# Two heads of scores ahead of each group's products, and four smaller moves, in a cross-attention kernel

## The chip, the cores and the metric

The kernel runs on one NeuronCore of one Trainium2 chip. The metric is the device time of one execution, in microseconds (us). Before the change it is 429.61 us, the median of three runs (429.59 to 430.12).

The engines are named as in the profile: PE is TensorE's matrix multiply and PEld its loading of weights, DVE is VectorE, ACT is ScalarE, POOL is GpSimd and SP is SyncE, which here only issues DMA transfers.

## The reference

Eight batches of 112 query rows with 320 channels attend to 375 context rows of 512 features, with 20 heads of 16 channels. The last four context rows are prompt tokens, with keys and values of their own. Cut to what matters:

```
q        = heads(x @ W_q)
probs_t  = softmax(q @ heads(text @ W_k)^T * scale)           # 371 text rows
text_out = probs_t @ heads(text @ W_v)
qsem     = l2norm(probs_t @ text)                             # 512 wide, per head
sem      = qsem @ l2norm(ip)^T                                # 4 prompt rows
fused    = q @ heads(ip @ W_k_ip)^T * scale + 0.5 * sem
probs_ip = softmax(fused) * spatial_mask
ip_out   = probs_ip @ heads(ip @ W_v_ip)
out      = (text_out + ip_out) @ W_out + b_out + x
```

## The kernel before, in words

All arithmetic is float32. A head is never expanded to 512 features: the norm of `qsem` comes from the Gram matrix of the context. For one head the kernel multiplies the unnormalised probabilities by a matrix `u` whose columns are a triangle of the Gram matrix, the four prompt columns, a column of ones and the head's 16 values. One product of up to 392 columns so gives, in one PSUM bank `ps_qd`, everything that the head needs.

The 40 steps are pairs (b, g) of a batch and a group of four heads. The four heads of a group use the four strips of 32 rows of TensorE's array, head `a` on strip `a`. A step consists of:

- `scores` (line 676): one product of 32 rows by 375 columns for a head, on the strip of that head, into a PSUM bank `ps_s`. In float32 each product appears as two instructions.
- `probabilities` (line 705): VectorE takes the negative maximum `nmx` (L709), ScalarE the exponential `p` (L712) and copies the prompt logits `ipl` (L714), and `sent` (line 718) has SyncE put `p` into another layout `xg`.
- `transposed` (line 725): VectorE transposes `xg` to `xgT` (L729).
- `multiplied` (line 735): twelve blocks (the index `j`) of four products (L748). After each block the generator yields, and other work is written in between.
- `value_sums` (L761, ScalarE) and `reduced` (L794, VectorE) read the four banks `ps_qd`, after which the next group may use them.

The loop over the steps (line 1207) works two steps ahead. During step n it writes the scores of heads 2 and 3 of step n + 2 (`now`) after block 0, and those of heads 0 and 1 (`then`) after block 6. Their probabilities follow at once for `now` and after the products for `then`. In two steps of the second to last batch other heads are also written after block 0 (`more`).

After the products of a step, `between(b, g)` (line 1079) writes pieces of the next batch's work: its Gram matrix, its values (`ps_v`, L578, copied by L585), its keys (`ps_k`, L544, copied by L551; the third chunk is transposed by L535 and copied by L540), the projected queries (`project_queries`: transposes L333, copies L336, projections L344, masked copies `qm` on VectorE, L353), and `finish` of the batch before (the transposes `ps_a`, L950, copied by L954, and the projection `ps_o`, L962). For the first batch `prompt_logits` (L665, copied by L672) belongs to these too.

PSUM has eight banks, dealt out in three pools: four for `ps_qd`, two for scores (`ps_sc`) and two common ones (`ps_mm`). `bank(name)` takes a common one and `bank(name, spare=True)` one of the two for scores. Each pool hands its banks out in turn, so a tile waits until the last reader of the tile two before it (in these pools of two) has finished.

The instructions of TensorE, SyncE, VectorE and (in the loop) ScalarE run in the order in which they are written; a wait in front of one holds back those that are written after it on its engine. GpSimd's are ordered by the planner. GpSimd's copy L655 (`placed`) puts a group's values `vr` into `u`; these come from DRAM (L603, `values_to_groups`, after step (b, 3)), where SyncE stored them (L594).

Of the kernel before, what the change touches and what calls it, by code (L numbers as in the profile page):

```python
# [20 lines left out]
def kernel(  # L21
# [16 lines left out]
    B, S, C = x.shape  # L38
# [10 lines left out]
    FULL = C // P  # L49
# [11 lines left out]
    NG = H // GROUP  # L61
# [23 lines left out]
    def bank(name, spare=False):  # L85

        if spare:
            return ps_sc.tile([P, 512], F32, tag="sc", name=name)
        return ps_mm.tile([P, 512], F32, tag="mm", name=name)
# [223 lines left out]
    pairs = [[0]] + [list(range(b, min(b + 2, B))) for b in range(1, B, 2)]  # L313
# [211 lines left out]
    def keys(b):  # L525
        s = st[b]
        if b > 0:
            nc.gpsimd.tensor_copy(s["kT"][:, :, TT:], kip[:, :, b * NIP : (b + 1) * NIP])
        for i in range(NC):
            ps = bank(f"ps_k_{b}_{i}", spare=0 < b < B - 1 and i == FULL)  # L530
            if 0 < b < B - 1 and i == FULL:

                for c in range(NT):
                    rows = min(P, TT - c * P)
                    nc.tensor.transpose(  # L535
                        ps[:, c * P : c * P + rows],
                        s["k3"][:rows, c].rearrange("p a r d -> p (a r d)"),
                        ident[:rows, :rows],
                    )
                nc.scalar.copy(s["kT"][:, i, :TT], ps[:, :TT])  # L540
                yield
                return
            for e in range(NE):
                nc.tensor.matmul(  # L544
                    ps[:, :TT],
                    wk_sb[:, e, i * P : (i + 1) * P],
                    s["ctxT"][:, e, :TT],
                    start=(e == 0),
                    stop=(e == NE - 1),
                )  # L550
            nc.scalar.copy(s["kT"][:, i, :TT], ps[:, :TT])  # L551
            yield
# [382 lines left out]
    def prompt_sums_and_projection(b, s, eng, part, n, h0, i0, i1, w, attn, ah):  # L935
        wv = work.tile([S, NIP, H, D], F32, tag="wv", name=f"wv_{b}_{h0}", bufs=1)[:, :, :n]
        eng.tensor_tensor(  # L937
            wv,
            s["vip"][:, :, part],
            w.rearrange("p h n -> p n h").unsqueeze(3).to_broadcast([S, NIP, n, D]),  # L940
            ALU.mult,
        )
        eng.tensor_tensor(wv[:, :2], wv[:, :2], wv[:, 2:], ALU.add)
        eng.tensor_tensor(ah, ah, wv[:, 0], ALU.add)
        eng.tensor_tensor(ah, ah, wv[:, 1], ALU.add)
        yield

        ps = bank(f"ps_a_{b}_{h0}", spare=True)
        for i in range(i0, i1):
            nc.tensor.transpose(  # L950
                ps[:, i * S : (i + 1) * S], attn[:, i * P : (i + 1) * P], ident[:S, :S]
            )
        aT = work.tile([P, NC, S], F32, tag="aT", name=f"aT_{b}_{h0}")
        nc.scalar.copy(  # L954
            aT[:, i0:i1], ps[:, i0 * S : i1 * S].rearrange("p (i s) -> p i s", s=S)
        )
        yield

        s["o"] = bank(f"ps_o_{b}")
        ps = s["o"]  # L960
        for i in range(i0, i1):
            nc.tensor.matmul(  # L962
                ps[:S, :C], aT[:, i, :], wo_sb[:, i, :], start=(i == 0), stop=(i == NC - 1)
            )
        yield
# [106 lines left out]
    def run(key, make, pieces=1):  # L1072

        if key not in gens:
            gens[key] = make()
        for _ in range(pieces):
            next(gens[key], None)

    def between(b, g):

        nb = b + 1
        new = nb < B


        first = [bs for bs in pairs if bs[0] == (nb if b == 0 else nb + 1)]
        rest = [bs for bs in pairs if bs[0] == nb]
        if g == 0:
            if new:
                run(("g", nb), lambda: gram(nb), 2)
            if new:  # L1090
                run(("g", nb), None)
            if b == 0:
                run(("v", nb), None)
            if b > 0 and new:
                run(("f", b - 1), lambda: finish(b - 1))
        if g == 1:
            if new:
                run(("v", nb), lambda: values(nb), 1 if b == 0 else 2)
            if b == 0:
                run(("pp",), prompt_projections)  # L1100
            for bs in first if b == 0 else ():
                run(("q", bs[0]), lambda: project_queries(bs), 3)
        if g == 2 and new:
            run(("v", nb), None)
            run(("k", nb), lambda: keys(nb))
            for bs in first if b == 0 else ():
                run(("q", bs[0]), None)
        if g == 2 and b > 0 and new:
            run(("f", b - 1), None, 2)
        if g == 3:  # L1110
            if new:
                run(("k", nb), None, 1)
            if b > 0 and new:
                run(("f", b - 1), None)
            for bs in first if b > 0 else ():
                run(("q", bs[0]), lambda: project_queries(bs), 3)
            if b == 0:
                run(("t", b), lambda: prompt_logits(b))
            for bs in rest:
                run(("q", bs[0]), None)  # L1120
        if g < NT and nb + 1 < B:
            run(("c", nb + 1), lambda: transposed_context(nb + 1))
        if g == 4:
            if b > 0 and new:
                run(("f", b - 1), None, 2)
            if nb < B - 1:
                run(("k", nb), None, 1)
            for bs in (first if b > 0 else []) + (rest if b < B - 2 else []):
                run(("q", bs[0]), None)

    prompts = normalised_prompts()
    context = transposed_context(0)
# [62 lines left out]
    def ahead(n):  # L1195

        c, d = steps[n + LEAD : n + LEAD + 2]
        if steps[n] == (B - 2, NG - 2):
            todo = ((c, 2, 3), (c, 0, 1), (d, 2, 3))
        elif steps[n] == (B - 2, NG - 1):  # L1200
            todo = ((c, 0, 1), (d, 2, 3), (d, 0, 1))
        else:
            todo = ((c, 2, 3), (c,), (c, 0, 1))
        return [[(t[0], a) for a in t[1:]] for t in todo]

    ctx.enter_context(tc.manual_schedule(engines=engines | {mybir.EngineType.Activation}))
    for n, (b, g) in enumerate(steps[:-NG]):
        now, more, then = ahead(n)
        for j, _ in enumerate(multiplied(b, g)):
            if j == 0:  # L1210
                for c, a in now:
                    scores(*c, a)
                    probabilities(*c, a)
                for c, a in more:
                    scores(*c, a, ps=bank(f"ps_s_{c[0]}_{c[1]}_{a}"))
                    probabilities(*c, a, hold=True)
            if j == 6:
                for c, a in then:
                    scores(*c, a)
            if j == 2:  # L1220
                if g == 0:
                    gram_banks(b + 1)
                transposed(*steps[n + 1])
                for c, a in more:
                    sent(*c, a)
                if 1 <= g <= 3:
                    gram_to_groups(b + 1, {1: (0,), 2: (2,), 3: (3,)}[g])

                if g in (1, 2) and b > 0:
                    run(("f", b - 1), None)  # L1230
        value_sums(b, g)
        if g == 2 and b > 0:
            run(("f", b - 1), None)
        for c, a in then:
            probabilities(*c, a)
        if n == len(steps) - NG - 1:
            sums = shared(b, g, GROUP // 2)
            next(sums)
            reduced(b, g, 2)
        else:  # L1240
            reduced(b, g)
        placed(*steps[n + 1])
        if g == 0 and b > 1:
            run(("f", b - 2), None)
        load_rest(n)
        if g == NG - 1:
            load_next(b + 3)
        if g == 1:
            gram_to_groups(b + 1, (1,))
        elif g == 3:  # L1250
            values_to_groups(b + 1)
        if g in (2, 3) and b == 0:
            run(("pp",), None)
        if (b, g) == (B - 3, 1):
            prompt_values_by_head()
        if (b, g) == (B - 2, 1):
            bd = load_prompt_values_by_head()
        if g == NG - 1 and b < B - 2:
            prompt_values(b)
        between(b, g)  # L1260
        if g == 1:
            values_to_dram(b + 1, nc.sync, 0, 2)
        if g == 2:
            values_to_dram(b + 1, nc.sync, 2)
# [10 lines left out]
    b = B - 1  # L1275
# [126 lines left out]
```

## Time and profile before

| | us |
|---|---|
| median of three runs | 429.61 |
| profiled execution | 429.75 |
| its span, first to last instruction | 428.0 |
| TensorE busy (share of the span) | 419.5 (98%) |
| VectorE busy | 327.8 (77%) |
| ScalarE busy | 189.7 (44%) |
| GpSimd busy | 111.1 (26%) |
| products `ps_qd`, busy time of TensorE | 221.7 |
| scores `ps_s` | 65.5 |
| values `ps_v` | 63.6 |
| keys `ps_k` (L544) | 46.3 |

A line of a timeline gives the start and the busy time in us, the engine, the line of the code, the operation, what it writes and reads, the size of the first of the instructions that the line merges and their count; in brackets stands the idle time of the engine before it and what ended it. A matmul is pipelined and its end is modelled, so a busy TensorE is not one at its peak. The view of the waits gives for a pair "who waits <- for whom" the sum in us, how many times, and the longest. The granted clock of TensorE was 0.999 of full speed.

### The profile page before, as it was taken

How to read it: one execution, taken by the hardware profiler on the slowest of the kernel's cores; microseconds unless marked ns; L12 is line 12 of the kernel's file. 1: busy time of each engine (PE TensorE's matmuls, PEld its weight loads, DVE VectorE, ACT ScalarE, POOL GpSimd, SP SyncE). 2: the span in 40 equal slices, each digit the busy share in tenths (PEclk: the TensorE clock that was granted, in tenths of full speed). 3: DMA queues.
4: the chain of work that ended last, by engine and by line, in shares of the span. 5: the costliest groups of instructions: out<-in, count | busy, mean ns of one | idle time of the engine just before them, and what ended most of it. 6: DMA issues, size and time to landing. Idle time of an engine off the chain costs nothing.

```text
span 428.0 us, 13975 instructions
## 1 busy us (share of the span) xinstructions
PE 419.5 (98%) x5521; PEld 330.3 (77%) x5521; DVE 327.8 (77%) x672; ACT 189.7 (44%) x659; POOL 111.1 (26%) x275
## 2 busy tenths in 40 slices
PE   8999999989999999999999999999999999999995
PEld 8867768878777877789777977788777887687993
DVE  5038569787887879788797878887788977889873
ACT  2344342346334353345435363334634363446773
POOL 5310101112060212411152121511133120515550
PEclk9999999999999999999999999999999999999999
DMA  8776665687645956476646956468556536564200
GB/s 239 199 192 211 140 169 157 160 200 149 166 123 138 207 152 179 123 162 150 168 121 160 189 124 170 127 153 175 141 166 153 145 96 173 156 159 121 65 2 27
DMA packets 57630, 64.26 MB, mean 150 GB/s; under 512 B 18448, under 2 KB 51592, under 8 KB 57566
## 3 DMA queue, kind: packets, MB, share of 16 engines
q1 hardware_dynamic: 56934, 62.42, 58.2%
q8 instruction: 43, 0.70, 0.8%
q10 hardware_dynamic: 632, 0.96, 0.7%
q14 instruction: 21, 0.17, 0.1%
HBM read 18.67 MB, written 5.32 MB: 56 GB/s over the span
## 4 chain that ended last, share of the span: by engine, by line
PE 90%; DVE 3%; ACT 3%; DMA 1%; issue 1%; POOL 0%; DVEq 0%; ACTq 0%
PE ps_qd L748 43%; PE ps_v L578 15%; PE ps_k L544 10%; PE ps_g L502 7%; PE ps_s L686 5%; PE ps_q L344 3%; PE ps_o L962 2%; PE ps_g L458 1%; DVE junk L794 1%; ACT shared L787 1%; DMA xg<-p 1%; DVE nmx L709 1%; DMA ct<-in_ctx_dram 1%; PE ps_k L560 1%; PE ps_c L417 1%
## 5 line engine op out<-in xcount | busy, mean ns | idle before, releaser
L748 PE MATMUL ps_qd<-u,xgT 32*112 32x168 f32 (+11 forms) x3840 | 221.7, 353 | 0.3 <-POOL u L655 0.3
L748 PEld LDWEIGHTS ps_qd<-u,xgT 32*112 32x112 f32 x3840 | 189.0, 172 | 33.7 <-issue 10.4
L729 DVE STREAM_TRANSPOSE xgT<-xg 128x1536 f32<-128x1536 f32 (+1 forms) x45 | 119.3, 2672 | 6.7 <-DMA xg<-p 6.7
L712 ACT ACTIVATE p<-ps_s,nmx 112x371 f32<-112x371 f32 x156 | 84.8, 582 | 74.8 <-DVE nmx L709 63.5
L709 DVE TENSOR_REDUCE nmx<-ps_s 112x1 f32<-112x371 f32 x160 | 77.5, 529 | 42.2 <-PE ps_s L686 41.3
L794 DVE CUSTOM_DVE_ANT_0 junk<-ps_qd,p 112x371 f32<-112x371 f32 x146 | 79.2, 542 | 17.4 <-PE ps_qd L748 1.4
L686 PE MATMUL ps_s<-kT,qm 32*112 32x375 f32 (+1 forms) x320 | 65.5, 484 | 0.1
L655 POOL COPY u<-vr 128x64 f32<-128x64 f32 x120 | 25.9, 238 | 152.4 <-PE ps_qd L748 100.9
L578 PE MATMUL ps_v<-wv_sb,ctxT 128*128 128x384 f32 (+1 forms) x192 | 63.6, 480 | 0.0
L578 PEld LDWEIGHTS ps_v<-wv_sb,ctxT 128*128 128x128 f32 x192 | 35.2, 190 | 19.7
L544 PE MATMUL ps_k<-ctxT,wk_sb 128*128 128x371 f32 x136 | 46.3, 483 | 0.2 <-DVE ctxT L425 0.2
L761 ACT COPY pvs<-ps_qd 112x21 f32<-112x21 f32 x151 | 16.3, 190 | 62.3 <-PE ps_qd L748 61.9
L544 PEld LDWEIGHTS ps_k<-ctxT,wk_sb 128*128 128x128 f32 x136 | 24.9, 190 | 15.2 <-POOL ct L138 0.5
L502 PE MATMUL ps_g<-ctxT 128*32 128x375 f32 (+11 forms) x672 | 30.4, 333 | 0.0
L686 PEld LDWEIGHTS ps_s<-kT,qm 32*112 32x112 f32 x320 | 26.7, 170 | 4.8 <-ACT kT L551 2.0
L502 PEld LDWEIGHTS ps_g<-ctxT 128*32 128x32 f32 x672 | 27.7, 110 | 2.0
L714 ACT COPY ipl<-ps_s 112x4 f32<-112x4 f32 x140 | 23.5, 168 | 0.0
L353 DVE TENSOR_SCALAR qm<-ps_q,emask 128x224 f32<-128x224 f32 (+1 forms) x25 | 9.0, 394 | 17.1 <-PE ps_q L344 17.1
L585 ACT COPY vext<-ps_v 128x384 f32<-128x384 f32 (+1 forms) x24 | 11.3, 469 | 22.4 <-PE ps_v L578 22.3
L404 DVE STREAM_TRANSPOSE ctxT<-ct 128x512 f32<-128x512 f32 x18 | 19.9, 1108 | 1.6 <-DMA ct<-in_ctx_dram 1.6
L475 POOL TENSOR_TENSOR ug<-ug,half 128x128 f32<-128x128 f32 (+1 forms) x24 | 10.5, 450 | 31.9 <-ACT ug L474 31.9
L937 POOL TENSOR_TENSOR wv<-vip,w 112x1280 f32<-112x1280 f32 x6 | 14.8, 2466 | 14.2 <-DVE w L877 14.2
(171 smaller groups left out, 323.8 us busy)
## 6 DMA issues: line engine op xcount, KB each, us to landing
xg<-p SPq DMA_DIRECT2D x156, 162.3 KB
u<-ug SPq DMA_DIRECT2D x124, 99.0 KB
ct<-in_ctx_dram SPq DMA_DIRECT2D x24, 176.0 KB
vr<-vd SPq DMA_DIRECT2D x32, 120.0 KB
vip<-vipd SPq DMA_DIRECT2D x6, 560.0 KB
vd<-vext SPq DMA_DIRECT2D x7, 320.0 KB
vd<-vext SPq DMA_DIRECT2D x7, 160.0 KB
out_dram<-ob SPq DMA_DIRECT2D x8, 140.0 KB
```

The source lines that it names most:

```text
L404: nc.vector.transpose(ctxT[:, :, c * P : (c + 1) * P].rearrange("p e (j i) -> p j e i", i=RG), ct[:, some, :].rearrange("p j (k e) -> p j ...
L502: nc.tensor.matmul(ps[c][q * RG : (q + 1) * RG, j * RG - c * P : T - c * P], ctxT[:, e, j * RG : (j + 1) * RG], ctxT[:, e, j * RG : T], st ...
L544: nc.tensor.matmul(ps[:, :TT], wk_sb[:, e, i * P : (i + 1) * P], s["ctxT"][:, e, :TT], start=(e == 0), stop=(e == NE - 1),)
L578: nc.tensor.matmul(ps[:, :w], ctxT[:, e, c * P : (c + 1) * P], wv_sb[:, e, :w], start=(e == 0), stop=(e == NE - 1),)
L655: nc.gpsimd.tensor_copy(v, dealt(b, c, s["vr"][:, c * QN : (c + 1) * QN, g, :]))
L686: nc.tensor.matmul(ps[:S, :w], qm[a * RG : (a + 1) * RG, i, r, j * S : (j + 1) * S], s["kT"][a * RG : (a + 1) * RG, i, :w], start=True, st ...
L709: nc.vector.tensor_reduce(nmx, ps[:S, :TT], AX.X, ALU.max, negate=True)
L712: nc.scalar.activation(s["p", g][:, a, :], ps[:S, :TT], AF.Exp, bias=nmx)
L714: nc.scalar.copy(s["ipl"][:, groups[g][a], :], ps[:S, TT:T])
L729: nc.vector.transpose(xT[:, j : j + n].rearrange("p j (k q) -> p q j k", q=QN), xg[:, :, j * RG : (j + n) * RG].rearrange("p q (j k) -> p ...
L748: nc.tensor.matmul(banks[a][:S, j * RG : UW], xT[a * RG : (a + 1) * RG, j, :S], region(b, c)[a * RG : (a + 1) * RG, q, j * RG - c * P :], ...
L794: nc.vector.tensor_tensor_reduce(out=junk, in0=ps[:S, :TT], in1=s["p", g][:, a, :], scale=1.0, scalar=0.0, op0=ALU.mult, op1=ALU.add, accu ...
```

## The change

Five edits, none of which adds or removes an instruction:

1. In the loop over the steps, the scores and probabilities of `now` (heads 2 and 3 of the step two ahead) are written before block 0 of the products, not after it. Four steps are excepted and stay as they were (`turned`): (0, 2), and (1, 4), (3, 4), (5, 4), which follow the transposes of a new pair of inputs.
2. After g = 2, the first piece of the next batch's keys is written before the last piece of its values.
3. `ps_a` takes a common bank, no longer one of the two for scores.
4. The third chunk of the keys of batch 1 takes a common bank; for batches 2 to 6 it stays with those for scores.
5. `prompt_logits` of the first batch moves from g = 3, ahead of the projected queries, to the end of g = 4.

```diff
@@ keys
-            ps = bank(f"ps_k_{b}_{i}", spare=0 < b < B - 1 and i == FULL)
+            ps = bank(f"ps_k_{b}_{i}", spare=1 < b < B - 1 and i == FULL)
@@ prompt_sums_and_projection
-        ps = bank(f"ps_a_{b}_{h0}", spare=True)
+        ps = bank(f"ps_a_{b}_{h0}")
@@ between
         if g == 2 and new:
+            run(("k", nb), lambda: keys(nb))
             run(("v", nb), None)
-            run(("k", nb), lambda: keys(nb))
             for bs in first if b == 0 else ():
                 run(("q", bs[0]), None)
@@ between, g == 3
             for bs in first if b > 0 else ():
                 run(("q", bs[0]), lambda: project_queries(bs), 3)
-            if b == 0:
-                run(("t", b), lambda: prompt_logits(b))
             for bs in rest:
                 run(("q", bs[0]), None)
@@ between, g == 4
             for bs in (first if b > 0 else []) + (rest if b < B - 2 else []):
                 run(("q", bs[0]), None)
+            if b == 0:
+                run(("t", b), lambda: prompt_logits(b))
@@ the loop over the steps
         now, more, then = ahead(n)
+        turned = (b, g) == (0, 2) or g == NG - 1 and any(bs[0] == b + 2 for bs in pairs)
+        if not turned:
+            for c, a in now:
+                scores(*c, a)
+                probabilities(*c, a)
         for j, _ in enumerate(multiplied(b, g)):
             if j == 0:
-                for c, a in now:
+                for c, a in now if turned else ():
                     scores(*c, a)
                     probabilities(*c, a)
                 for c, a in more:
```

## The prediction

> **What bounds the kernel now.** First the page, for the shares of the engines and the chain that ended last.
>
> ```profile
> span 428.0 us, 13975 instructions
> ...
> PE 419.5 (98%) x5521; PEld 330.3 (77%) x5521; DVE 327.8 (77%) x672; ACT 189.7 (44%) x659; POOL 111.1 (26%) x275
> ...
> PE 90%; DVE 3%; ACT 3%; DMA 1%; issue 1%; POOL 0%; DVEq 0%; ACTq 0%
> ```
>
> TensorE has work in 98% of the span and carries 90% of the chain; VectorE is next with 77%. So an edit is worth only what it gives back of TensorE's own stalls. The view of the waits says who waits for whom (us in total, times, longest).
>
> ```profile
> DVE nmx L709 <- PE ps_s L686: 41.3, 35, 3.4
> ...
> PEld ps_s L686 <- ACT kT L551: 2.0, 6, 0.3
> ...
> PEld ps_qd L748 <- DVE ss L794: 1.6, 4, 0.7
> ```
>
> The largest wait that the change can touch is VectorE's for the scores, 41.3 us. But VectorE is not the bound, and its idle time is not time of the kernel. TensorE's own waits for others come to a few us. They do not all show as idle time, because four strips of the array run at once. So I read them from the length of a group's products, from its first product to the next work on TensorE. An ordinary group, (3,2), in the timeline of TensorE (start us, us, then the group of instructions):
>
> ```profile
> 208.75 1.22 PE L748 MATMUL ps_qd<-u,xgT 32*112 32x392 f32 x10
> 209.51 0.48 PE L686 MATMUL ps_s<-kT,qm 32*112 32x375 f32 x2
> ...
> 209.83 0.48 PE L686 MATMUL ps_s<-kT,qm 32*112 32x375 f32 x2
> ...
> 214.11 1.24 PE L578 MATMUL ps_v<-wv_sb,ctxT 128*128 128x384 f32 x3
> ```
>
> It lasts 214.11 - 208.75 = 5.36 us. One block of products is 8 instructions (four heads, two passes each), yet x10 run before the first score, which is written after 8: heads 0 and 1, on strips that the scores of heads 2 and 3 do not use, are already in the next block. One pass of a score costs its strip 209.83 - 209.51 = 0.32 us, so a score 0.64 us, on its own strip alone. With the scores put first, strips 2 and 3 do them first and strips 0 and 1 begin their products at once. Each strip has the same work in either order, so **an undisturbed group stays at 5.36 us** and 31 such moves (35 groups less the four left as they were) give nothing by themselves. Only groups that are longer have something to return.
>
> ```profile
> 88.74 1.32 PE L748 MATMUL ps_qd<-u,xgT 32*112 32x392 f32 x9
> ...
> 94.82 4.34 PE L502 MATMUL ps_g<-ctxT 128*32 128x375 f32 x96
> ```
> ```profile
> 138.42 1.22 PE L748 MATMUL ps_qd<-u,xgT 32*112 32x392 f32 x10
> ...
> 143.98 1.45 PE L502 MATMUL ps_g<-ctxT 128*32 128x375 f32 x17
> ```
> ```profile
> 158.97 1.22 PE L748 MATMUL ps_qd<-u,xgT 32*112 32x392 f32 x9
> ...
> 164.79 2.85 PE L578 MATMUL ps_v<-wv_sb,ctxT 128*128 128x384 f32 x8
> ```
> ```profile
> 286.68 1.22 PE L748 MATMUL ps_qd<-u,xgT 32*112 32x392 f32 x10
> ...
> 292.30 1.13 PE L502 MATMUL ps_g<-ctxT 128*32 128x375 f32 x12
> ```
> ```profile
> 335.71 1.56 PE L748 MATMUL ps_qd<-u,xgT 32*112 32x392 f32 x7
> ...
> 342.04 4.34 PE L502 MATMUL ps_g<-ctxT 128*32 128x375 f32 x96
> ```
>
> Over 5.36 us: (1,0) 0.72, (2,0) 0.20, (2,2) 0.46, (5,0) 0.26, (6,0) 0.97; (3,0) and (4,0) lie between the first and the last of their kind, 0.20 each. **Together 3.0 us.** Their cause stands at the head of the group:
>
> ```profile
> 335.15 0.47 ACT L540 COPY kT<-ps_k 128x371 f32<-128x371 f32 x1 [0.67 <-PE ps_k L535]
> ...
> 336.69 0.17 PEld L748 LDWEIGHTS ps_qd<-u,xgT 32*112 32x112 f32 x1 [0.70 <-DVE ss L794]
> ```
>
> The fourth head's product waits until VectorE has read that head's bank of the last group (L794), and the scores stand behind it in the queue though they need nothing of that bank.
>
> **The change part by part.** *Scores ahead of the products.* No instruction is added. In (6,0) the scores fill strips 2 and 3 for 0.64 us while the fourth bank is awaited; strip 3 then idles 0.98 - 0.64 = 0.34 and strips 0 and 1, whose first block takes about 0.75 (two passes, 208.75 to 209.51), 0.23. I take a return of 0.65 of 0.97. In (2,2) and the four short ones the wait is under 0.64, so all of it comes back: 0.46 + 0.86. The lower bound is nothing (the bank is awaited anyway and the wait is merely later), the upper all 3.0.
>
> What is new is that the scores' waits now stand at the head, with 96 products behind them on all four strips. They need a score bank, the keys' copy and the queries. The bank: at (6,0) the last reader of one is the copy of 335.15, which ends at 335.62, 0.09 before TensorE arrives; in the other batches two batches' queries (1.31, a row of 87.50 below) stand between that copy and the group, and I take nothing. The keys' copy already delays scores by 2.0 us in six places, covered there by products; moving the keys' first chunk ahead of the last values puts a values chunk of some 2.7 us between, so this stays covered and costs nothing. The queries cost something in (0,3) alone, where they are projected just before.
>
> ```profile
> 70.51 1.28 PE L748 MATMUL ps_qd<-u,xgT 32*112 32x392 f32 x10
> 70.62 0.81 DVE L353 TENSOR_SCALAR qm<-ps_q,emask 128x224 f32<-128x224 f32 x2 [0.60 <-PE ps_q L344]
> ...
> 71.19 0.20 PEld L686 LDWEIGHTS ps_s<-kT,qm 32*112 32x112 f32 x2 [0.39 <-issue]
> ```
>
> Scores that come first wait until 71.19 rather than start at 70.51: 0.68, with all strips idle, less the 0.08 by which that group is long now (its next work is the row of 75.95 below): +0.60. If both halves of L353 were needed it would be +0.85; if VectorE came earlier, +0.3.
>
> *The first batch's logits and keys.*
>
> ```profile
> 66.69 2.76 PE L544 MATMUL ps_k<-ctxT,wk_sb 128*128 128x371 f32 x8
> ...
> 75.95 2.76 PE L544 MATMUL ps_k<-ctxT,wk_sb 128*128 128x371 f32 x8
> 78.55 0.67 PE L665 MATMUL ps_ip<-kipb,qT 128*112 128x32 f32 x6
> ...
> 80.61 1.22 PE L748 MATMUL ps_qd<-u,xgT 32*112 32x392 f32 x10
> ...
> 87.12 0.54 PE L535 MATMUL ps_k<-ident,k 128*128 128x128 f32 x3 [1.08 <-ACT ipl L714]
> 87.50 1.31 PE L344 MATMUL ps_q<-xT,wq_sb 128*128 128x224 f32 x6
> ```
>
> Without the logits the stretch after (0,3), now 80.61 - 75.95 = 4.66, becomes keys and queries alone, as after (0,2): 70.51 - 66.69 = 3.82, so -0.84. After (0,4) the keys' third chunk no longer waits 1.08 for a score bank, but the logits (0.67) come last and take the bank of that chunk, third in a pool of two, so they wait for its copy.
>
> ```profile
> 87.42 0.17 ACT L714 COPY ipl<-ps_s 112x4 f32<-112x4 f32 x1
> ...
> 87.63 0.59 POOL L655 COPY u<-vr 128x64 f32<-128x64 f32 x3 [1.83 <-DMA vr<-vd]
> ```
>
> ScalarE comes to it at 87.59, copies 0.47, and the logits end near 88.06 + 0.05 + 0.67 = 88.78, as late as now (88.74). Without that wait it would be 0.45 better. The group (1,0) is then held by GpSimd's u, now ready at 88.22 and later by the 0.60 of (0,3), since its load is issued behind that group's transfers: 88.82, while TensorE comes at 88.74 - 0.24. Products from 88.85 on, no stall after: 88.85 + 5.36 = 94.21 against 94.82. For the first batch I take **-0.60**.
>
> *ps_a in the two common banks.* After (b,3) the order is keys' second chunk, ps_a, then queries (even b) or transposed inputs (odd b). The third of them now gets the bank of the first and waits for its copy.
>
> ```profile
> 178.03 0.45 PE L950 MATMUL ps_a<-ident,attn 112*128 112x112 f32 x3
> ...
> 178.23 0.47 ACT L551 COPY kT<-ps_k 128x371 f32<-128x371 f32 x1 [1.15 <-PE ps_k L544]
> ...
> 178.32 1.31 PE L344 MATMUL ps_q<-xT,wq_sb 128*128 128x224 f32 x6
> ```
> ```profile
> 129.47 0.38 PE L333 MATMUL ps_x<-ident,x_sb 112*64 112x112 f32 x2 [0.23 <-ACT aT L954]
> ```
> ```profile
> 383.81 0.27 PEld L748 LDWEIGHTS ps_qd<-u,xgT 32*112 32x112 f32 x2 [0.45 <-POOL u L655]
> ```
>
> In even batches the queries go from 178.32 to about 178.70 + 0.1: +0.5 for b = 2, 4 and 6, of which 0.45 in batch 6 falls into the wait for u before (7,0). In odd batches a wait for the copy replaces the present one for the copy of aT: nothing. Bounds: 0 if the banks fall otherwise, 3.0 if all six batches pay.
>
> *Keys ahead of values* also puts the last values' copy and their store after the keys' copy; both stand on ScalarE and SyncE ahead of exponentials that come later anyway, and the values are read back a whole group later: nothing, at most the 0.5 of one copy in each of six batches if the first exponentials queue behind it. *Earlier scores* bring VectorE's maxima, the exponentials and SyncE's sends forward by one block, 0.76 us. SyncE issues in the order of the program, so the loads behind them go earlier too. This loosens VectorE; I count no time for it.
>
> The sum: -0.60 (first batch) - 0.46 - 0.86 - 0.65 (stalls) + 1.0 + 0.05 (banks) = **-1.5 us**. The profiled execution took 429.75 (its span 428.0 and 1.75 around it), so 428.2; the median of the runs, 429.61, is 0.14 lower: **428.1 us**.
>
> **The rivals.** *More comes back (426.4).* All 3.0 us of stalls return, the first batch's edits give -0.24 and the banks cost nothing: -3.25. For it: VectorE gets its scores 0.76 earlier and releases banks earlier. Against: the row of 178.23 shows the copy just where the queries want its bank.
>
> *Nothing to be seen (429.4).* Half of the stalls (1.3) stay because VectorE's last read of a bank still sets the head of the group. For it: the row of 336.69 names that read, and the scores do not move it. Against: the scores are exactly what can run meanwhile.
>
> *Slower (431.9).* The wait for the keys' copy decides. Place: between the second keys' chunk and the next user of its bank after (b,3). Price: 0.5 in each of six batches, +3.0, less 0.45 in the last and 0.24 from the first batch, +2.3, if the heads' stalls return nothing because TensorE, later by 0.5, finds VectorE as late as before. It decides once the stalls return less than 2.3. Against: in odd batches the row of 129.47 shows a wait of like size that goes away.
>
> *Strict order on TensorE (449).* If two passes on one strip held back other strips, each moved pair would idle strips 0 and 1 for 0.64 us: 31 x 0.64 = +20. The x10 in the row of 208.75 speaks against it. The Trainium skill, "TensorE: Matmul & The Clock Gate", Part 3 (The mechanism), says that matmuls start and end strictly in program order; by that rule this rival would hold, and the trace does not agree.
>
> **How the numbers follow.** A measurement of this kernel can tell about 0.2%, 0.86 us, from no change. Chances: forecast 0.50, more 0.14, nothing 0.17, slower 0.17, strict order 0.02. Faster: 0.50 + 0.14 = 0.64; same 0.17; slower 0.19. The forecast's own range, with the bounds of the bank waits and of the stalls' return, is 427.3 to 428.8. The range takes in the case of no change and most of the larger gain: 426.7 to 430.1.
>
> **What would show it.** Right: ordinary groups still 5.36 us; (1,0), (2,2), (3,0) at 5.4; (6,0) at 5.7; a new wait of 0.4 to 0.5 of L344 for the keys' copy in even batches; a wait of 0.6 for L353 at the head of (0,3); VectorE's wait for scores down from 41.3 by some 20 us with little for the kernel in it. Wrong: ordinary groups longer than 5.36; a wait for ScalarE at the head of many groups; stalls for L794 as long as now.

## The result and the profile after

The changed kernel takes 427.99 us (median of five runs, 427.76 to 429.28). The kernel before, run beside it, takes 430.12 (five runs, 429.59 to 431.05). The ratio is 0.9962 with a 95% interval of 0.9949 to 0.9976: faster, by 1.0 to 2.2 us. The forecast was 428.1, worked out from a kernel before of 429.61; the two medians here differ by 2.1 us, where the sum had 1.5.

First the page of the changed kernel: its span, the busy engines, the chain that ended last.

```profile
span 427.6 us, 13996 instructions
...
PE 417.4 (98%) x5521; PEld 326.8 (76%) x5521; DVE 327.4 (77%) x672; ACT 188.7 (44%) x659; POOL 110.9 (26%) x275
...
PE 83%; DMA 5%; DVE 5%; ACT 4%; issue 1%; SPq 1%; POOL 0%; DVEq 0%; ACTq 0%
```

TensorE is as full as before, and the work is the same. But the chain now runs through transfers for 5% of the span, against 1% before. The profiled execution took 429.28 us, which is the longest of the five; the other four lie at 427.76 to 428.02. So its trace holds about 1.3 us that the others don't have, and each stall in it has to be looked for in a second trace before it is put down to the kernel.

The view of the waits (us in total, times, longest), of all engines:

```profile
DVE nmx L709 <- PE ps_s L686: 24.6, 21, 3.4
...
DVE xgT L729 <- DMA xg<-p: 17.5, 10, 3.8
...
PEld ps_x L333 <- ACT kT L551: 2.0, 3, 1.1
...
PEld ps_q L344 <- ACT kT L551: 1.4, 3, 0.5
...
PEld ps_qd L748 <- DVE ss L794: 1.3, 3, 0.4
```

VectorE's wait for scores fell from 41.3 us to 24.6, while its wait for the rearranged probabilities `xg` rose from 6.7 us (eight times) to 17.5 (ten times, at most 3.8). The scores come earlier and the transfers do not come earlier by as much, so a good part of the idle time only changed its name.

An ordinary group, (3,2), in TensorE's timeline (start us, us, then the instructions), for comparison with the same group before:

```profile
208.19 0.57 PE L686 MATMUL ps_s<-kT,qm 32*112 32x375 f32 x2
208.20 0.58 PE L748 MATMUL ps_qd<-u,xgT 32*112 32x392 f32 x2
208.60 0.48 PE L686 MATMUL ps_s<-kT,qm 32*112 32x375 f32 x2
...
213.55 1.20 PE L544 MATMUL ps_k<-ctxT,wk_sb 128*128 128x371 f32 x3
```

Scores and products start within 0.01 us of each other although the scores are written ahead: they are on different strips. From the first product to the next work are 213.55 - 208.20 = 5.35 us, against 5.36 before. The scores cost nothing and return nothing here.

The places that the prediction named, in the timeline of the changed kernel (rows of three engines, by time):

```profile
70.43 0.81 DVE L353 TENSOR_SCALAR qm<-ps_q,emask 128x224 f32<-128x224 f32 x2 [0.61 <-PE ps_q L344]
71.02 0.57 PE L686 MATMUL ps_s<-kT,qm 32*112 32x375 f32 x2 [0.64 <-DVE qm L353]
71.04 0.58 PE L748 MATMUL ps_qd<-u,xgT 32*112 32x392 f32 x2
...
87.56 0.76 PE L665 MATMUL ps_ip<-kipb,qT 128*112 128x32 f32 x6 [0.30 <-ACT kT L540]
...
88.27 0.58 PE L748 MATMUL ps_qd<-u,xgT 32*112 32x392 f32 x2
...
93.69 1.76 PE L502 MATMUL ps_g<-ctxT 128*32 128x375 f32 x21
...
177.15 0.45 PE L950 MATMUL ps_a<-ident,attn 112*128 112x112 f32 x3
177.35 0.47 ACT L551 COPY kT<-ps_k 128x371 f32<-128x371 f32 x1 [1.24 <-PE ps_k L544]
177.88 1.40 PE L344 MATMUL ps_q<-xT,wq_sb 128*128 128x224 f32 x6 [0.27 <-ACT kT L551]
...
336.41 0.67 PE L748 MATMUL ps_qd<-u,xgT 32*112 32x392 f32 x2
...
341.85 1.51 PE L502 MATMUL ps_g<-ctxT 128*32 128x375 f32 x18
```

At (0,3) all strips wait 0.64 us for the masked queries. (1,0) lasts 93.69 - 88.27 = 5.42 us (6.08 before), (6,0) 341.85 - 336.41 = 5.44 (6.33 before). In batch 2, `ps_a` ends before the queries can start, because their bank is the one that the keys' copy of 177.35 still reads.

Two groups are longer than the prediction allowed, (2,2) and (5,4):

```profile
152.71 2.98 DVE L729 STREAM_TRANSPOSE xgT<-xg 128x1536 f32<-128x1536 f32 x1 [3.82 <-DMA xg<-p]
...
157.71 0.68 PE L748 MATMUL ps_qd<-u,xgT 32*112 32x392 f32 x2
...
158.51 0.27 PEld L748 LDWEIGHTS ps_qd<-u,xgT 32*112 32x112 f32 x2 [0.43 <-DVE ss L794]
...
163.92 1.51 PE L544 MATMUL ps_k<-ctxT,wk_sb 128*128 128x371 f32 x4
...
321.84 2.99 DVE L729 STREAM_TRANSPOSE xgT<-xg 128x1536 f32<-128x1536 f32 x1 [2.45 <-DMA xg<-p]
...
327.19 1.60 PE L748 MATMUL ps_qd<-u,xgT 32*112 32x392 f32 x9
...
328.21 0.17 PEld L748 LDWEIGHTS ps_qd<-u,xgT 32*112 32x112 f32 x1 [0.43 <-DVE ss L794]
...
333.56 1.87 PE L962 MATMUL ps_o<-wo_sb,aT 128*112 128x320 f32 x6
```

(2,2) lasts 163.92 - 157.71 = 6.21 us and (5,4) 333.56 - 327.19 = 6.37. The rows are of the same kind in both. A transfer of `xg` lands late, the transpose L729 waits for it, and everything behind it on VectorE is late by as much, the last reads L794 of the four banks among it. Those banks are what the next group's products want.

For the experiments one table, worked out from the traces' instructions. "Length" is from a group's first product to the modelled end of its last (0.08 us more than the measure above), "gap" from that end to the first product of the next group. The first column is the end of (1,0) counted from the first product of (0,0).

| kernel | end of (1,0) | gap to (2,3) | gaps to (2,4), (4,4), (6,4) | gaps to (1,4), (3,4), (5,4) | (3,0) | (2,2) | (5,4) | (6,0) |
|---|---|---|---|---|---|---|---|---|
| before | 57.81 | 5.20 | 4.06, 4.06, 3.58 | 3.90, 3.90, 3.81 | 5.63 | 5.89 | 5.83 | 6.40 |
| after | 56.88 | 5.22 | 4.60, 4.59, 4.13 | 3.98, 3.98, 4.29 | 5.42 | 6.28 | 6.43 | 5.51 |
| again | 56.79 | 5.21 | 4.60, 4.59, 4.13 | 3.98, 3.97, 3.69 | 5.42 | 5.42 | 6.43 | 5.58 |
| edit 1 alone | 57.65 | 5.94 | 4.08, 4.08, 3.71 | 3.91, 3.90, 3.81 | 5.42 | 5.42 | 5.44 | 5.81 |
| edits 2 to 5 | 57.62 | 5.20 | 4.58, 4.58, 4.10 | 3.97, 3.98, 3.69 | 5.64 | 5.67 | 6.10 | 6.26 |
| edits 1, 2 | 57.65 | 5.21 | 4.08, 4.07, 3.71 | 3.90, 3.90, 4.13 | 5.42 | 5.42 | 6.31 | 5.51 |
| all but edit 3 | 56.79 | 5.21 | 4.07, 4.07, 3.71 | 3.90, 3.90, 3.81 | 5.42 | 5.42 | 6.22 | 5.51 |
| no exceptions | 57.62 | 5.21 | 4.59, 4.60, 4.13 | 4.68, 4.68, 4.35 | 5.42 | 6.05 | 5.42 | 5.51 |

### The profile page after: what moved, and what is told of

It is laid out like the page before. It is cut to its first block, busy times and chain, and to the rows that moved or that the text cites. A ratio compares the mean times of both kernels' runs of the same rounds, so it can differ in the third digit from the quotient of the medians.

```text
span 427.6 us, 13996 instructions
## 1 busy us (share of the span) xinstructions
PE 417.4 (98%) x5521; PEld 326.8 (76%) x5521; DVE 327.4 (77%) x672; ACT 188.7 (44%) x659; POOL 110.9 (26%) x275
## 4 chain that ended last, share of the span: by engine, by line
PE 83%; DMA 5%; DVE 5%; ACT 4%; issue 1%; SPq 1%; POOL 0%; DVEq 0%; ACTq 0%
PE ps_qd L748 36%; PE ps_v L578 12%; PE ps_k L544 9%; PE ps_s L686 9%; PE ps_g L502 6%; PE ps_q L344 3%; DMA xg<-p 3%; PE ps_o L962 3%; DMA vipx<-vipd 2%; DVE xgT L729 1%; PE ps_g L458 1%; ACT p L712 1%; ACT shared L787 1%; DMA ip_sb<-in_ctx_dram 1%; PE ps_x L333 1%
## 5 line engine op out<-in xcount | busy, mean ns | idle before, releaser
L729 DVE STREAM_TRANSPOSE xgT<-xg 128x1536 f32<-128x1536 f32 (+1 forms) x45 | 119.5, 2674 | 18.2 <-DMA xg<-p 17.5
L709 DVE TENSOR_REDUCE nmx<-ps_s 112x1 f32<-112x371 f32 x160 | 77.2, 527 | 26.6 <-PE ps_s L686 24.6
L794 DVE CUSTOM_DVE_ANT_0 junk<-ps_qd,p 112x371 f32<-112x371 f32 x146 | 79.3, 543 | 17.9 <-PE ps_qd L748 1.4
L686 PE MATMUL ps_s<-kT,qm 32*112 32x375 f32 (+1 forms) x320 | 66.4, 496 | 0.7 <-DVE qm L353 0.6
L686 PEld LDWEIGHTS ps_s<-kT,qm 32*112 32x112 f32 x320 | 23.8, 170 | 12.7 <-issue 10.3
L714 ACT COPY ipl<-ps_s 112x4 f32<-112x4 f32 x140 | 24.4, 174 | 0.0
```

Source lines behind the costliest of these rows:

```text
L686: nc.tensor.matmul(ps[:S, :w], qm[a * RG : (a + 1) * RG, i, r, j * S : (j + 1) * S], s["kT"][a * RG : (a + 1) * RG, i, :w], start=True, st ...
L709: nc.vector.tensor_reduce(nmx, ps[:S, :TT], AX.X, ALU.max, negate=True)
L714: nc.scalar.copy(s["ipl"][:, groups[g][a], :], ps[:S, TT:T])
L729: nc.vector.transpose(xT[:, j : j + n].rearrange("p j (k q) -> p q j k", q=QN), xg[:, :, j * RG : (j + n) * RG].rearrange("p q (j k) -> p ...
L794: nc.vector.tensor_tensor_reduce(out=junk, in0=ps[:S, :TT], in1=s["p", g][:, a, :], scale=1.0, scalar=0.0, op0=ALU.mult, op1=ALU.add, accu ...
```

## The experiments

The experiments ran in three sets, each with the kernel before on the same chip. Set 1 (430.04 us before): the changed kernel once more, edit 1 alone, edits 2 to 5, edit 3 undone. Set 2 (430.35): edits 1 and 2, no exceptions, the copy elsewhere, two more places. Set 3 (429.81): the last three. The ratios are against the kernel before of the set.

**The changed kernel once more.** No edit; it shows which of the two long groups belongs to the kernel.

> The changed kernel once more, to see what of its profiled execution (429.3 us, against 427.8 to 428.0 in its other runs) comes back. In that execution the products of (2,2) lasted 6.28 us and those of (5,4) 6.43, because the transpose two steps of work earlier waited 3.82 and 2.45 us for xg to land. Theory A (transfers are the floor there: SyncE's loads of vip and x fill the DMA engines around 138 to 152 us, in every execution): (2,2) again 5.9 to 6.3. Theory B (one late transfer in one execution): both near 5.4. I expect A for (2,2) and B for (5,4), and a time of 428.0.

427.67 us (427.03 to 428.30), ratio 0.9943 (0.9928 to 0.9957). The two transposes ahead of the long groups, in its timeline:

```profile
151.44 2.98 DVE L729 STREAM_TRANSPOSE xgT<-xg 128x1536 f32<-128x1536 f32 x1 [2.30 <-DMA xg<-p]
...
320.61 2.99 DVE L729 STREAM_TRANSPOSE xgT<-xg 128x1536 f32<-128x1536 f32 x1 [1.84 <-DMA xg<-p]
```

In batch 2 the transfer is late by 2.30 us and (2,2) is back at 5.42; in batch 5 it is late by 1.84 and (5,4) is still 6.43. So (2,2) has a slack that 2.30 us do not use up and 3.82 do. Its loss is not in every execution, though two later kernels show it again (3.62 us late and 6.05 long in both). (5,4) has less slack and loses in both traces of this kernel. The expectation had the two places the wrong way round.

**Edit 1 alone**, on the kernel before:

```diff
+        turned = ...     # as in the full change
+        if not turned:
+            for c, a in now:
+                scores(*c, a)
+                probabilities(*c, a)
...
-                for c, a in now:
+                for c, a in now if turned else ():
```

> Edit 1 alone (scores of now ahead of the products, same four exceptions) on the kernel before. Mine (TensorE's stalls): the heads of (b,3) now wait for the copy of the keys' first chunk, written last before them, about 0.6 us in each of six batches, +3.6; (0,3) +0.6; stalls at the heads return 1.9 to 2.5; no bank waits. In all 431.0, between 430 and 432. Rival (VectorE's earlier start is what pays): 427.5 to 428.5, since VectorE's wait for the scores falls in the same way.

430.75 us (430.46 to 431.25), ratio 1.0015 (1.0005 to 1.0025): no gain, rather a loss. The stalls at the heads of groups are gone as in the full change ((3,0) 5.42, (2,2) 5.42, (6,0) 5.81), and six new ones take their place. The view of its waits and, below it, the head of (2,3) in its timeline:

```profile
PEld ps_s L686 <- ACT kT L551: 6.9, 6, 1.2
```
```profile
167.17 2.66 PE L544 MATMUL ps_k<-ctxT,wk_sb 128*128 128x371 f32 x8
170.38 0.57 PE L686 MATMUL ps_s<-kT,qm 32*112 32x375 f32 x2 [0.56 <-ACT kT L551]
```

The scores need the copy of the keys' first chunk, which is written just before them. Behind eight products that wait was covered; at the head of the group it stands ahead of 96 products, and the gap grows from 5.20 to 5.94 us, 6 x 0.74 = 4.4 us in all. That is more than the heads had to return. VectorE's earlier start does not pay for it, so the rival falls.

**Edits 1 and 2 alone**:

```diff
         if g == 2 and new:
+            run(("k", nb), lambda: keys(nb))
             run(("v", nb), None)
-            run(("k", nb), lambda: keys(nb))
```

> Edits 1 and 2 alone on the kernel before (ps_a, the third keys of batch 1 and the first batch's logits as before). Against edit 1 alone (430.75) the heads of (b,3) no longer wait for the keys' copy: six gaps of 5.94 us become 5.21, -4.4. So 426.4, between 426.0 and 427.2, and the first batch ends as late as with edit 1 alone. Rival (the other moves are needed for the gain): 428 or more.

427.02 us (426.50 to 429.10), ratio 0.9932 (0.9908 to 0.9956). With a piece of the values between the keys and the scores the gap is 5.21 again. Edit 2 is therefore what makes edit 1 pay: 1.0015 without it, 0.9932 with it, some 3.6 us. Of the 4.4 us that the six gaps return, (5,4) and the gap ahead of it take back 0.87 + 0.32, and (6,0) returns 0.30 more. Within the noise these two edits bring all that the full change brings; its ratio in set 1 was 0.9943.

**Edits 2 to 5 without edit 1**:

```diff
-        turned = (b, g) == (0, 2) or g == NG - 1 and any(bs[0] == b + 2 for bs in pairs)
+        turned = True
```

> Edits 2 to 5 without edit 1 (scores stay after block 0 everywhere). Mine: the first batch gains about 0.8 after (0,3) and some of its 1.1 us wait for a score bank, the even batches lose 3 x 0.54 to the wait of L344 for the keys' copy, the head stalls stay: 430.0, between 429.3 and 431. Rival (the small moves bring the gain, edit 1 nothing): 428.

430.99 us (429.74 to 431.69), ratio 1.0020 (1.0009 to 1.0030). The heads keep their stalls ((3,0) 5.64, (6,0) 6.26) and the queries' waits for the bank are there (4.58 for 4.06). So the gain of the whole needs edit 1. The first batch shows the same: its end comes at 57.62 here and at 57.65 with edit 1 alone (57.81 before), but at 56.88 with the full change. Here the logits (L665) wait 0.92 us for the copy L540, and the products then wait for `u`.

**Edit 3 undone** in the changed kernel:

```diff
-        ps = bank(f"ps_a_{b}_{h0}")
+        ps = bank(f"ps_a_{b}_{h0}", spare=True)
```

> The changed kernel with edit 3 taken back (ps_a in a bank for scores again). Mine: the wait of L344 for the keys' copy in the even batches goes (3 x 0.54), the odd ones wait for aT in place of the keys' copy, about 0: 426.6, between 426.2 and 427.2, unless the transfers give part of it back. Rival (edit 3 is needed, because scores at the head would wait for ps_a's reader in a bank for scores): 428.5 or more, with L686 waiting for ACT L954.

426.03 us (425.52 to 427.76), ratio 0.9911 (0.9894 to 0.9928), about 1.6 us under the full change in the same set and a little under the range that was expected. The even batches' gaps fall back to 4.07, 4.07 and 3.71 and no score waits for `ps_a` in exchange. Edit 3 alone costs what the prediction feared of it.

**No exceptions**: the scores come first in all steps.

```diff
-        turned = (b, g) == (0, 2) or g == NG - 1 and any(bs[0] == b + 2 for bs in pairs)
+        turned = False
```

> The changed kernel without the four exceptions: scores ahead of the products in all 35 steps. Mine: at (0,2) and at (1,4), (3,4), (5,4) the head waits for ScalarE's copies of the transposed inputs, which hold both banks for scores: (0,2) +0.4, (1,4) and (3,4) +0.5 each, (5,4) between -0.3 and +0.5, since VectorE is late there anyway. In all +1.4 on 427.7 to 428.0: 429.2, between 428.5 and 429.8. Rival (the exceptions hide nothing, strips 0 and 1 go on meanwhile): 427.8 as with them.

429.86 us (429.38 to 431.00), ratio 0.9989 (0.9974 to 1.0004), a little above the range that was expected: against the 0.9943 of the changed kernel the four exceptions are worth about 2 us, if the two sets may be compared. In its timeline, at the head of (1,4):

```profile
128.71 0.79 PE L333 MATMUL ps_x<-ident,x_sb 112*128 112x112 f32 x6 [0.27 <-ACT kT L551]
129.80 0.80 PE L686 MATMUL ps_s<-kT,qm 32*112 32x375 f32 x2 [0.30 <-ACT xT L336]
130.14 0.59 PE L748 MATMUL ps_qd<-u,xgT 32*112 32x392 f32 x2
```

There the scores want a bank that the copy L336 of the transposed inputs reads, and the gap grows from 3.98 to 4.68. The head of (5,4), where VectorE is late, gains by the same move (5.42 for 6.43), but its gap grows.

**The copy of the prompt values elsewhere.** The late transfer of batch 5 comes after a copy from DRAM to DRAM (L618, 200 KB, SyncE's queue) that `prompt_values_by_head` issues after (5,1). Here, on top of edit 3 undone, it is issued one batch earlier:

```diff
-        if (b, g) == (B - 3, 1):
+        if (b, g) == (B - 4, 1):
             prompt_values_by_head()
```

> The changed kernel with ps_a back in a bank for scores (426.0 in the last comparison) and the copy of the last batches' prompt values into vipx issued one batch earlier, after (4,1). Theory: the small packets of that copy (80 of 5 KB, drawn out over 5 us) sit in front of the transfers of xg for (5,3), whose transpose waits 1.75 us for them; this makes VectorE late at the head of (5,4), the products of which last 6.22 us. Moved, (5,4) is 5.44 to 5.6, and (4,4), where scores come first, at most 0.2 longer: 425.3, between 424.9 and 425.6. Rival (the transfers of xg are as late without it): (5,4) stays above 6.1, 426.0.

426.58 us (425.57 to 427.85), ratio 0.9913 (0.9890 to 0.9936): no gain over edit 3 undone alone. (5,4) is 5.44, as expected, but the late transfer has moved along, in the timeline of this kernel:

```profile
270.78 2.98 DVE L729 STREAM_TRANSPOSE xgT<-xg 128x1536 f32<-128x1536 f32 x1 [2.65 <-DMA xg<-p]
```

The gap to (4,4) is 4.78 for 4.07 and that to (5,0) 3.89 for 3.21. The expectation had taken the wait in batch 4 to be covered. It also counted 80 packets of the copy; the trace of edit 3 undone has 40 of 5 KB, from 307.7 to 313.0 us.

**Two more places**, on top of that one: (0,3) joins the exceptions, and the third transposed input `ps_x` of the later pairs takes a common bank.

```diff
-        turned = (b, g) == (0, 2) or ...
+        turned = (b, g) in ((0, 2), (0, 3)) or ...
...
-                ps = bank(f"ps_x_{bs[0]}_{i}", spare=i > 0)
+                ps = bank(f"ps_x_{bs[0]}_{i}", spare=i == 1 or i > 1 and bs[0] == 1)
```

> As the last, and two more edits against waits that the runs showed: (0,3) joins the exceptions (its scores waited 0.6 us at the head for the masked queries), and the third transposed input of the later pairs takes a common bank, where it waits for the keys' copy and no longer for aT's (0.23, 0.23 and 0.42 us). Expected: 425.3 - 0.6 - 0.5 = 424.2, between 423.7 and 424.9. Rival (TensorE comes earlier but VectorE and the transfers do not follow): 425.3, with longer waits for L794 at the heads of groups.

425.72 us (424.58 to 426.91), ratio 0.9894 (0.9870 to 0.9918). The ratio is the lowest so far, but its interval overlaps those of the two kernels before it in which edit 3 is undone, and the time lies above the range that was expected (423.7 to 424.9). The bank of `ps_x` returns 0.34 in each odd batch (gaps 3.56, 3.56 and 3.47). At (0,3) the gap falls from 4.65 to 3.93, but it is given back before (1,0):

```profile
87.50 0.76 PE L665 MATMUL ps_ip<-kipb,qT 128*112 128x32 f32 x6 [0.89 <-ACT kT L540]
...
269.42 3.00 DVE L729 STREAM_TRANSPOSE xgT<-xg 128x1536 f32<-128x1536 f32 x1 [1.89 <-DMA xg<-p]
```

The logits wait 0.89 us where they waited 0.30, and (1,0) ends at 56.86 as in the full change. The transfer of batch 4 is late again, by 1.89, and this time covered: (4,4) lasts 5.47 with a gap of 4.07.

**Three last ones** on top of this kernel: the copy of the prompt values issued after (6,0) and its load after (6,3); edit 5 undone; both.

```diff
-        if (b, g) == (B - 4, 1):
+        if (b, g) == (B - 2, 0):
             prompt_values_by_head()
-        if (b, g) == (B - 2, 1):
+        if (b, g) == (B - 2, 3):
             bd = load_prompt_values_by_head()
```
```diff
@@ between, g == 3
+            if b == 0:
+                run(("t", b), lambda: prompt_logits(b))
             for bs in rest:
                 run(("q", bs[0]), None)
@@ between, g == 4
-            if b == 0:
-                run(("t", b), lambda: prompt_logits(b))
```

> e8 with the copy of the prompt values from DRAM to DRAM (L619) issued after (6,0), and the load of its result (L630) after (6,3). Theory: that copy draws out the transfer of probabilities that follows it by a few groups, wherever it is issued, and between (6,0) and (6,3) the other loads of SyncE are done, so that TensorE has slack: (4,4) and (5,4) both 5.4 to 5.5 with the gaps ahead of (4,4) and (5,0) at 4.07 and 3.21, and the time within 0.5 us of e8's (425.2 to 426.2), since e8's execution already shows 5.47 and 5.44 there; VectorE's wait of L729 for xg falls from 12.2 us by 1 to 4. Rival: the copy is not the cause, the transfers are late at these places whatever is issued there: (5,4) is again 5.8 or more and the time 0.4 to 1 us above e8's.

> e8 with edit 5 undone (the first batch's prompt logits back at g=3, ahead of the second part of the queries). Theory: what (0,3) gained in e8 was given back at the wait of the logits L665 for the keys' copy L540 because the logits stand last ahead of (1,0); with them a block earlier that wait goes, (0,4) to (1,0) falls from 3.21 to about 2.3 to 2.6, the gap ahead of (0,4) grows from 3.77 to 4.2 to 4.6 (the logits' own time), and (1,0) starts at 87.7 to 88.2 us: the time 0 to 0.5 us under e8's. Rival: (1,0) is held by the input u of its products or by the keys' copy wherever the logits stand: it starts at 88.2 to 88.6 and the time is not under e8's.

> e9's and e10's edits together on e8. Theory: both are places apart, so their effects add: the time is e8's plus the two differences, 424.9 to 426.2. Rival: they interact through the transfers of probabilities: 0.5 us or more away from the sum.

| | us | ratio |
|---|---|---|
| copy after (6,0) | 424.80 (424.29 to 428.02) | 0.9886 (0.9859 to 0.9914) |
| edit 5 undone | 425.48 (425.15 to 426.83) | 0.9896 (0.9878 to 0.9913) |
| both | 425.33 (425.09 to 425.90) | 0.9890 (0.9873 to 0.9907) |

The three ratios and the 0.9894 of the kernel that they start from can't be told apart, so whether the two effects add can't be said either. All four kernels beat both the kernel before and the changed one. With the copy after (6,0), in both kernels that have it there, no transpose that runs during a fourth group waits for its transfer in batches 1 to 6. With edit 5 undone the wait of the logits is gone, but in the trace of that kernel (1,0) is held by GpSimd's `u`:

```profile
88.95 0.58 POOL L655 COPY u<-vr 128x64 f32<-128x64 f32 x3 [2.85 <-DMA xg<-p]
89.24 3.08 PE L748 MATMUL ps_qd<-u,xgT 32*112 32x392 f32 x37 [0.40 <-POOL u L655]
```

There (1,0) ends at 57.28, against 56.86 with edit 5, as the rival says. But the kernel with both edits runs the same program up to (4,1), and in its trace `u` is in time and another wait takes its place, the one for VectorE's last read:

```profile
87.46 0.59 POOL L655 COPY u<-vr 128x64 f32<-128x64 f32 x3 [1.71 <-DMA vr<-vd]
...
89.24 2.80 PEld L748 LDWEIGHTS ps_qd<-u,xgT 32*112 32x112 f32 x47 [0.43 <-DVE ss L794]
```

(1,0) starts earlier there, lasts 6.08 us and ends at 56.69. So the rival is not shown: the first batch has several things that are ready at almost the same time, and which of them holds (1,0) differs from one execution to the next.

The profiled execution of "copy after (6,0)" took 428.02 us, while four of that kernel's six runs took 424.29 to 425.08. It can be set beside the trace of the kernel that it starts from, whose program is the same up to (4,1); the spans differ by 3.2 us (426.3 and 423.1). Three things make this up. `u` comes late, which widens the gap ahead of (1,0) from 3.21 to 4.31:

```profile
89.30 0.58 POOL L655 COPY u<-vr 128x64 f32<-128x64 f32 x3 [3.23 <-DMA xg<-p]
```

(1,0) itself lasts 7.03 us for 5.53. For 3.4 us of it TensorE is granted half its clock, which by an estimate from that (half of 3.4) costs 1.7 us. The view by stretches shows it (the clock is the third number from the end):

```profile
89.40:92.80 3.40, 3.23 (x23) 3.16 (x25) 1.61 (x4) 1.56 (x6) 0.77 (x4) 0.50 0.95 212
```

And (2,2) is 0.63 longer (6.05 for 5.42), after a transfer that is 3.62 us late.

## Why the prediction was right, step by step

**Undisturbed groups unchanged: right.** 5.35 us for 5.36. Over the 31 moves nothing shows of the 20 us of strict order. That rival, which the Trainium skill's page "TensorE: Matmul & The Clock Gate" supports by its rule, has fallen.

**The stalls at the heads return: right, and rather more than taken.** The four short ones, (2,0) to (5,0), are at 5.42 by the table's measure (5.63 to 5.69 before), 0.90 for the 0.86 of the forecast. (6,0) returned 0.89 (0.82 in the second trace) where 0.65 was taken. The wait of products for VectorE's reads (L794) is 1.3 us in the first trace and 0.4 in the second, for 1.6 before. (2,2) returned its 0.46 in eight of the eleven traces with edit 1; in the profiled execution of the change a single late transfer made it longer instead. That execution's 6.28 and the wider gap to (5,4) (4.29 for 3.69 in the second trace) are 0.86 + 0.60 us, about what it lies above the other runs (1.3).

**(0,3) waits for the queries: right.** +0.60 was forecast; the gap grew by 0.72 and the group got 0.09 shorter, +0.63.

**First batch: right in sign, mis-sized.** -0.60 was forecast, the end of (1,0) came 0.93 earlier. The step that failed is the floor: `u` was to be later by the 0.60 of (0,3) and ready at 88.82. It was not, as GpSimd's row in the timeline of the changed kernel shows:

```profile
87.29 0.59 POOL L655 COPY u<-vr 128x64 f32<-128x64 f32 x3 [1.81 <-DMA xg<-p]
```

It was ready at 87.88, and (1,0) started at 88.27, right after the logits. The stretch after (0,3) shrank from 4.58 to 3.77 as the sum had it (-0.81 for -0.84). When `u` is ready differs by more than the 0.60 between executions: from the first product of (0,0), it is 51.0 us in this trace, and 51.0 and 52.7 in two others ("two more places" and "copy after (6,0)") whose programs agree with each other up to (4,1).

**Banks: right in mechanism, too small.** In even batches the queries do wait for the keys' copy, +0.54, +0.53 and +0.55 at their gaps. The sum had 1.0 since 0.45 of batch 6 was to fall into the wait for `u`; that wait moved along instead (weight loads in the timeline, 0.45 us before and after) and the gap to (7,0) is 1.73 in both:

```profile
384.12 0.75 PEld L748 LDWEIGHTS ps_qd<-u,xgT 32*112 32x112 f32 x9 [0.45 <-POOL u L655]
```

So about 1.6 were paid, which is also what undoing edit 3 returned. In batch 7, (7,0) returned 0.32, which the prediction did not have (6.29 before, 5.97 after). It is 5.96 or 5.97 in every trace with edit 1 and 6.28 in edits 2 to 5, so it comes with edit 1; which wait it is was not tried. From (7,1) to (7,2) it is 5.99 us before, 5.69 after and 5.85 in the second trace. In odd batches one wait took the place of another, +0.08 in batches 1 and 3.

**Edit 2 costs nothing: right**, and the run without it showed what the cover is worth, 4.4 us.

**Earlier scores bring nothing by themselves: right** in that VectorE's wait for them fell by 17 us without a gain of that size. What the prediction left out is where this idle time goes: into the wait for transfers, and at (5,4) into the kernel. (5,4) is one of the exceptions, and the sum has no term for it. It grew by 0.60, in the first trace and in the second. Edit 1 alone, where the transpose waits 0.94 us, keeps it at 5.44; edits 2 to 5, with 0.83 but without scores put first, have 6.10.

As measured in the second trace, the stalls return 2.2 us, the first batch 1.0 and batch 7 0.5, and the banks take 1.6 and (5,4) 0.6: together -1.4, which is the difference of the spans (426.6 and 428.0). The forecast had -2.0, -0.6, nothing, +1.0 and nothing. So the mechanism was right, but that the sum came out so close is luck: the mis-sized first batch and banks and the missing (5,4) and batch 7 nearly cancel. It is luck too that the time agrees to 0.1 us, since the kernel before was 0.5 slower in the comparison than the 429.61 that the sum started from. The medians fell by 2.1 and, in set 1, 2.4 us; what the faster executions save beyond the traces stays open.

The rival "slower" had the right price for the bank wait (0.5 in each even batch) and the wrong condition: the stalls returned more than 2.3 us.

## What to carry to other kernels

Work that needs nothing of a late bank belongs ahead of the work that does, if it is on other strips and its own inputs have been ready for a while. Whether they have been is decided by what is written just before: here edit 2 made edit 1 worth some 3.6 us more. A step that is moved to the head of a queue has to be priced by the waits that it brings there, place by place, and exceptions at four places of 35 were worth about 2 us.

## What the runs showed of the hardware

**A small copy from DRAM to DRAM held up SyncE's queue until it had landed.** The copy L618 of 200 KB takes SyncE 0.68 us to issue. In all eight traces with its place after (5,1), the transpose that runs during (5,3) waits, 0.70 to 2.45 us (in six of them the profile names the transfer, in two nothing), while the same transposes of batches 1 to 4 wait at most 0.28; in the three kernels that issue it after (4,1), that of batch 4 waits (2.65, 1.89 and 1.47 us) and that of batch 5 does not; after (6,0), none. In the changed kernel and in the one with the copy a batch earlier, the rows of the issue (duration in ns, start in us):

```profile
L618 SPq DMA_DIRECT2D vipx<-vipd x1: 680/680/680, 308.4 to 308.4; - x1
```
```profile
L618 SPq DMA_DIRECT2D vipx<-vipd x1: 679/679/679, 257.7 to 257.7; - x1
```

How the lateness comes about stands in the changed kernel's view of SyncE's waits and in the view of the chain (start us, us, what):

```profile
SPq L721 <- DMA vipx<-vipd: 1.9, 1, 1.9
```
```profile
308.38 7.55 DMA vipx<-vipd
...
315.99 4.93 DMA xg<-p
```

The copy lands 7.55 us after its issue, and SyncE's next send of probabilities (L721) stands until then, although ScalarE had ended the exponentials of both heads at 314.45. It is issued at 315.99, 1.50 us before the first product of (5,3); in batch 4 the same send is issued 3.54 us before that of (4,3). The view names this wait in all eleven traces with the copy after (5,1) or (4,1), 0.7 to 1.9 us, and in neither of the two with it after (6,0). So the transfer is late because it is issued late. In most kernels with edit 1 the transpose waits longer than SyncE did, by up to 1.4 us; that part is not explained. Nor is it shown why a send of `p` waits for a copy with which it shares no data. The Trainium skill's page "DMA: Bandwidth & Descriptors", section "Queues, rings and completion order", says that SyncE has one ring on each transfer engine and that descriptors are taken in the order of the ring; the delay here arises before the ring, and no run here shows that rule. Whether another queue for this copy would help was not tried.

**Single late transfers and a lower clock make the executions of one kernel differ.** Two traces of the changed kernel differ at (2,2) by 0.86 us, where the transpose waited 3.82 us for its transfer in one and 2.30 in the other, with a mean granted clock of 1.0 in both. In the profiled execution of "copy after (6,0)" TensorE was granted half its clock from 89.41 to 92.82 us, and (1,0) is 1.5 us longer; no other of the thirteen traces has such a stretch before the last few us. Its other long run, 427.96 us, has the lowest mean clock of the six (0.994), but no trace. The places that lose are those where VectorE or GpSimd has little slack. What makes a transfer late in one execution and not in the next stays open, and so does what lowered the clock.
